# Thirteen gathered chunks are brought row by row by SyncE instead of by GpSimd

## The chip, the cores and the metric

The kernel runs on one core of one Trainium2 chip. The metric is the device time of one execution in microseconds. The engines are called PE (TensorE), DVE (VectorE), ACT (ScalarE), POOL (GpSimd) and SP (SyncE). Here SP does nothing but issue DMAs and read numbers into its registers. Each engine takes its instructions strictly in the order in which they were written.

## The reference

A graph of N = 6250 nodes and E = 100000 edges (`src`, `dst`, sorted by `dst`) passes through two layers of a graph isomorphism network, then a residual addition and a layer norm. Node features are 256 wide, hidden ones 512 wide, all in float32.

```python
def _gin_agg(h, src, dst, eps, n_nodes):
    agg = jax.ops.segment_sum(h[src], dst, num_segments=n_nodes)
    return (1.0 + eps) * h + agg

h = _gin_agg(x, src, dst, eps1, n)
h = jax.nn.relu(h @ W1a + b1a)
h = jax.nn.relu(h @ W1b + b1b)
h = _gin_agg(h, src, dst, eps2, n)
h = jax.nn.relu(h @ W2a + b2a)
out = h @ W2b + b2b
x = _layernorm(x + out, axis=-1)
```

## The kernel before

The edges are cut into chunks of 128. The destinations are skewed towards low node numbers, so the work is split in two. The seven node tiles of 128 nodes with the most edges ("heavy") are summed as matrix products: a table of counts (how many edges lead from one node to another) times the rows of all nodes. For all other chunks the 128 source rows are gathered, and a one-hot matrix on PE adds them up by destination.

**Gathers.** One chunk is one indirect DMA on POOL (`gather`, line 507): 128 rows of 1 KB from `x` in layer 1, 128 rows of 2 KB from `h1` (layer 1's result, in DRAM; `h` or `h_60` in the rows) in layer 2. They land in a ring of six pieces of up to four chunks each (`early`, in layer 2 also `late`), so that POOL can be 24 chunks ahead of the sums. PE adds a chunk up at line 1172; the merged sum of a group goes through `split` (lines 1216 to 1226) and a second product (line 1235), and DVE adds it to the tile's sum (`acc`, line 1245).

**Heavy tiles.** In layer 2 the counts come back from DRAM one table at a time (`ci<-counts`, line 1557, five buffers), ACT casts each into `cf` (line 1571, four buffers), the rows of four node tiles come as `xr<-h` (1 MB, line 1460) and are halved by ACT and DVE (lines 1532 to 1537), PE multiplies (line 1644), and DVE adds to `whole_acc` (line 1589). The heavy tiles' own rows come as `sown<-h` through one buffer (`sowing`), and DVE adds them at line 1622; each `sown` load waits until DVE is done with the one before it.

**Dense part.** Each block of node tiles is transposed (line 1289), goes through two products (lines 1342 and 1375) and is stored; in layer 2 its residual rows come as `r<-in_x` and its result goes out as `out_dram<-r`. The start value of a tile that is summed by gathers comes as `acc<-h` and is scaled by ACT (line 1002).

**Order.** A planner at build time (`Plan`) plays the engines with costs and writes the instructions of each engine in the order that comes out. It knows PE, DVE, ACT and POOL; an issue on SP costs nothing in it. SP's order is the order in which the planner came to each transfer.

**Row by row.** In layer 1 the last chunk of four groups is not gathered by POOL. SP reads 16 source numbers into registers (two `TENSOR_LOAD`s, line 2092), issues 16 DMAs of one row each into `b2b_c` (line 2098), rests in the plan for 14 us, and so on until 128 rows are there; the next chunk waits for the sum of the one before it.

```python
            def ferrying():
                yield ("rest", FERRY[0])
                n = FERRY[3]
                for g in ferries:
                    c = members[g][-1][0]
                    for o in range(0, P, n):
...
                        for j, v in enumerate(rows_in):
                            nc.sync.dma_start(b2b_c[o + j : o + j + 1, :], x[bass.ds(v, 1), :])
                        yield ("rest", FERRY[1])
```

Every DMA that SP or ACT issues takes the next of eight completion semaphores in turn, and waits until the DMA that had this one before has landed.

## Time and profile before

| what | value |
|---|---|
| time, median of 3 runs | 1304.05 us (1303.57 to 1305.85) |
| time of the profiled execution | 1301.3 us |
| its span, first to last instruction | 1299.5 us |
| busy PE / DVE / ACT / POOL | 1186.0 / 877.5 / 621.5 / 954.9 us |
| gathers on POOL | 490 in layer 1, 494 in layer 2 |
| row DMAs on SP | 512, all in layer 1 |
| mean granted PE clock | 0.962 of 2.4 GHz |

The span is what the profile shows; the device time of the same execution is 1.8 us longer. All rows and sums here are of this one execution, which is 2.75 us below the median. Busy time alone says little, because PE and POOL are both busy through most of the span; what counts is who waits for whom in which stage. SP has no busy time in the profile, as its issues are not counted, so it is read from its own timeline.

### The profile page before, as it was taken

The page shows a single profiled execution, that of the slowest core. Times are in us where ns is not written, and L with a number is a line of the kernel's source. Part 1 is how long each engine was busy: PE and PEld are TensorE (multiplying, and loading weights), DVE is VectorE, ACT ScalarE, POOL GpSimd, SP SyncE. Part 2 cuts the span into 40 slices and gives each one's busy share as a digit, 9 for nine tenths or more (in the row PEclk, how much of TensorE's full clock was granted, in tenths as well). Part 3 has the DMA queues.
Part 4 walks back from the last instruction along what each step waited for, and adds up shares of the span by engine and source line. Part 5 has one row for each costly group of instructions (what it writes and reads, how often), then busy time and mean ns, then how long its engine had stood idle before and what let it go on. Part 6 is the DMA issues. An engine that isn't in the chain of part 4 may idle for free.

```text
span 1299.5 us, 20725 instructions
## 1 busy us (share of the span) xinstructions
PE 1186.0 (91%) x6125; PEld 768.3 (59%) x6125; DVE 877.5 (68%) x2085; ACT 621.5 (48%) x1140; POOL 954.9 (73%) x997
## 2 busy tenths in 40 slices
PE   6879888889889989899788999899999999999987
PEld 4445455555455545455445677667776676766667
DVE  7997985878687979832156787678866665644334
ACT  6227766467646654674264453434343444432212
POOL 6777777777777777777777677777777777777770
PEclk9889999999999999899789899899999999999999
DMA  7446666567666665776599998898898899877771
GB/s 219 151 142 211 198 201 203 180 209 226 190 186 208 206 215 163 240 247 204 185 343 340 318 313 257 268 292 279 268 312 274 296 299 301 295 245 236 244 229 39
DMA packets 161978, 306.35 MB, mean 236 GB/s; under 512 B 26137, under 2 KB 94127, under 8 KB 161860
## 3 DMA queue, kind: packets, MB, share of 16 engines
q0 software_dynamic: 63040, 193.79, 47.9%
q1 hardware_dynamic: 77866, 86.72, 20.4%
q10 hardware_dynamic: 20954, 24.45, 5.4%
q8 instruction: 52, 0.85, 0.3%
q14 instruction: 66, 0.54, 0.1%
HBM read 274.42 MB, written 30.44 MB: 235 GB/s over the span
## 4 chain that ended last, share of the span: by engine, by line
PE 48%; DMA 17%; DVE 14%; ACT 8%; issue 6%; POOL 3%; SPq 2%; ACTq 1%; DVEq 1%; POOLq 0%
PE bank L1342 13%; PE bank L1375 10%; PE bank L1644 9%; PE bank L1172 7%; PE bank L1235 4%; DVE at L2074 3%; PE bank L1783 3%; DMA ci<-counts 3%; DMA late<-h,places 2%; DMA acc<-h 2%; DVE acc L1245 2%; DMA counts<-ci 2%; POOL early L507 2%; DVE cb L1857 2%; PE bank L1889 2%
## 5 line engine op out<-in xcount | busy, mean ns | idle before, releaser
L507 POOL DMA_INDIRECT early<-in_x_dram,srcs x490 | 481.5, 983 | 152.8 <-issue 132.0
L507 POOL DMA_INDIRECT early<-h,places x238 | 226.7, 953 | 75.4 <-issue 63.7
L507 POOL DMA_INDIRECT late<-h,places x232 | 221.9, 956 | 72.1 <-issue 57.3
L1245 DVE SCALAR_TENSOR_TENSOR acc<-bank,mask,acc 128x256 f32<-128x256 f32 (+1 forms) x360 | 205.1, 605 | 47.2 <-PE bank L1235 44.3
L1375 PE MATMUL bank<-w1b_s,ht 128*128 128x512 f32 (+1 forms) x392 | 188.8, 608 | 1.4 <-ACT ht L1352 0.8
L1342 PE MATMUL bank<-zt,w2a_s 128*128 128x256 f32 (+2 forms) x736 | 154.8, 364 | 0.2 <-ACT zt L1301 0.2
L1172 PE MATMUL bank<-early,sel 128*32 128x256 f32 (+1 forms) x1480 | 130.8, 468 | 24.1 <-DMA early<-h,places 8.5
L1644 PE MATMUL bank<-upper,cf 128*128 128x512 f32 (+1 forms) x343 | 148.8, 434 | 1.9 <-ACT upper L1532 1.1
L1342 PEld LDWEIGHTS bank<-zt,w2a_s 128*128 128x128 f32 x736 | 131.2, 193 | 24.1 <-issue 4.2
L1644 PE MATMUL bank<-xr,cf 128*128 128x512 f32 (+1 forms) x343 | 137.4, 401 | 1.1 <-DVE xr L1537 1.1
L2074 DVE TENSOR_TENSOR at<-bank,at 128x490 f32 x174 | 115.8, 666 | 28.3 <-ACT cf L1731 16.4
L1235 PE MATMUL bank<-split,to 128*128 128x256 f32 (+3 forms) x340 | 104.1, 426 | 18.8 <-DVE split L1226 6.9
L1026 DVE TENSOR_TENSOR sel<-iota,slot 128x256 f32<-128x256 f32 (+2 forms) x116 | 50.7, 437 | 98.4 <-PE bank L1172 95.0
L1375 PEld LDWEIGHTS bank<-w1b_s,ht 128*128 128x128 f32 (+1 forms) x392 | 74.2, 193 | 72.0 <-issue 60.7
L1342 PE MATMUL bank<-zt,w1a_s 128*128 128x256 f32 (+2 forms) x432 | 106.1, 397 | 9.4 <-ACT ht L1352 5.4
L1571 ACT CAST cf<-ci 128x512 fp32r<-128x512 uint16 (+1 forms) x91 | 54.1, 595 | 125.6 <-PE bank L1644 103.3
L1783 PE MATMUL bank<-xh,cf 128*128 128x512 f32 (+1 forms) x343 | 103.6, 438 | 9.3 <-DVE xh L1710 9.2
L1889 PE MATMUL bank<-cb,ca 128*128 128x490 f16 x288 | 86.0, 389 | 19.9 <-DVE at L2074 8.2
L1342 PEld LDWEIGHTS bank<-zt,w1a_s 128*128 128x128 f32 x432 | 84.2, 214 | 33.4 <-ACT ht L1352 6.3
L1172 PEld LDWEIGHTS bank<-early,sel 128*32 128x32 f32 x1480 | 40.2, 111 | 106.6 <-issue 62.5
L1710 DVE TENSOR_TENSOR xh<-bank,xh 128x512 fp32r<-128x512 f32 (+1 forms) x100 | 66.8, 672 | 43.1 <-ACT bank L1708 43.0
L1857 DVE TENSOR_SCALAR cb<-numbers,spot 128x490 f16<-128x490 f16 x288 | 90.7, 356 | 6.6 <-PE bank L1889 6.4
(193 smaller groups left out, 1764.0 us busy)
## 6 DMA issues: line engine op xcount, KB each, us to landing
raw<-in_x_dram SPq DMA_DIRECT2D x48, 512.0 KB
h<-h1r ACTq DMA_DIRECT2D x48, 256.0 KB
xr<-h SPq DMA_DIRECT2D x11, 1024.0 KB
counts<-ci ACTq DMA_DIRECT2D x84, 128.0 KB
ci<-counts SPq DMA_DIRECT2D x84, 128.0 KB
acc<-h SPq DMA_DIRECT2D x18, 512.0 KB
b2b_c<-in_x_dram SPq DMA_DIRECT2D x512, 1.0 KB
early<-in_x_dram,srcs POOLq DMA_INDIRECT x490
```

Source lines behind the costliest of these rows:

```text
L507: nc.gpsimd.indirect_dma_start(out=rows_[:, j, :], out_offset=None, in_=table, in_offset=bass.IndirectOffsetOnAxis(ap=rows_in[:, c - first ...
L1172: mm = nc.tensor.matmul(pm[b * SLOTS : (b + 1) * SLOTS], sel[:, c - groups[g][0], :], rows_[:, l, :], start=(c == part[0]), stop=(c == par ...
L1235: nc.tensor.matmul(pu[:, i * width : (i + 1) * width], to[:used], split[:used, l, :], start=(once or l == 0), stop=(once or l == 1),)
L1245: nc.vector.scalar_tensor_tensor(acc[t], pu[:, i * width : (i + 1) * width], mask[:, t - lo[g], g : g + 1], acc[t], op0=ALU.mult, op1=ALU.add,
L1342: nc.tensor.matmul(ph[:, (f - o) * TILES * P : (f - o) * TILES * P + nb], wa[:, k, f * P : (f + 1) * P], zt[:, k, :nb], start=(k == 0), st ...
L1375: nc.tensor.matmul(po[:m], ht[:, f, i * P : i * P + m], wb[:, f, :], start=(f == 0), stop=(f == KH - 1),)
L1644: nc.tensor.matmul(bank[token.number][:, :width], cf[:m, j, :], of[:m, j, :], start=(j == 0 and of is upper), stop=(j == len(ks) - 1 and o ...
L1710: begun_with["halves"] = nc.vector.tensor_tensor(xh[:m, two, 1, :], ap, xh[:m, two, 0, :], op=ALU.subtract)
L1783: nc.tensor.matmul(bank[tokens[i].number][:, : 2 * width], cf[:m, j, :], xh[:m, j, :, :].rearrange("p a d -> p (a d)"), start=(k == 0), st ...
L1857: made = nc.vector.tensor_scalar(token.tile, numbers, spot[:, c : c + 1], None, op0=ALU.is_equal)
L1889: mm = nc.tensor.matmul(bank[token.number][:, : NT * W], a.tile[:, c % BATCH, :], b.tile, start=(j == 0), stop=(j == n - 1),)
L2074: nc.vector.tensor_tensor(to, bank[token[0].number][:, : NT * W].rearrange("p (k w) -> p k w", w=W), to, op=ALU.add,)
```

## The change

- Layer 1: six chunks instead of four come row by row. 32 numbers are read at a time instead of 16, and the rest in the plan is 20 us for 32 rows instead of 14 us for 16.
- Layer 2: seven chunks, which POOL gathered before, come row by row in 28 batches of 32 rows of 2 KB from `h1`. They land by turns in the first 512 columns of `srcs` and of `dstf`, which hold the sources and destinations and are not read by layer 2. Their row numbers are first copied from `places2` to a small DRAM tile `rows2` by seven DMAs.
- So that the general path (taken when the data breaks a bound) still finds them, both tiles are stored to DRAM (`lent`) after layer 1, 256 KB each, and read back on that path alone.
- POOL issues 488 gathers in layer 1 and 487 in layer 2. PE does the same sums as before.

```diff
@@ -48,7 +48,9 @@
 PATIENT = 16.0
 SOWN2 = 25.0
 WEIGHT2 = 4.0
-FERRY = (45.0, 14.0, 5.0, 16, 610.0)
+FERRY = 32, 20.0, 5.0
+FERRY_FROM = (40.0, 5.0)
+FERRY_TO = (612.0, 596.0)
 LEAD = 1.5
 LATE = (6, 8)
 HASTE = -20.0
@@ -465,20 +467,30 @@
     FORETOLD = range(min(lo[g] for g in FORES), max(hi[g] for g in FORES) + 1)
     orders = {1: list(reversed(range(BEGIN[0], NG)))}
     orders[2] = FORES + [g for g in reversed(range(BEGIN[1], NG)) if g not in FORES]
-    ferries, t, free = [], FIRST, FERRY[0]
-    for g in orders[1]:
-        n = len(members[g])
-        t += GATHERS[0] * n
-        ready = free + FERRY[1] * P / FERRY[3] + FERRY[2]
-        if ready <= t + LANDINGS[0] and t < FERRY[4] and members[g][-1][0] < full:
-            ferries.append(g)
-            t -= GATHERS[0]
-            free = t + LANDINGS[0] + FERRY[2]
+    ferries = {}
+    for number, order in orders.items():
+        ferries[number], free = [], [FERRY_FROM[number - 1]] * number
+        t, until = (FIRST, HASTE)[number - 1], FERRY_FROM[number - 1]
+        for g in order:
+            t += GATHERS[number - 1] * len(members[g])
+            ready = max(until, free[0]) + FERRY[1] * P / FERRY[0]
+            if (
+                ready + FERRY[2] <= t + LANDINGS[number - 1] and t < FERRY_TO[number - 1]
+                and members[g][-1][0] < full and not (number == 2 and g in FORES)
+            ):
+                ferries[number].append(g)
+                t -= GATHERS[number - 1]
+                until = ready
+                free = free[1:] + [t + LANDINGS[number - 1] + FERRY[2]]
+    rows2 = dram.tile([len(ferries[2]), P], I32, name="rows2")
+    lent = [
+        (t[:, :H], dram.tile([P, H], t.dtype, name=f"lent{i}")) for i, t in enumerate((srcs, dstf))
+    ]
     pieces = {
         number: [
             (g, chunks[i : i + BURST])
             for g in order
-            for chunks in [members[g][: -1 if number == 1 and g in ferries else None]]
+            for chunks in [members[g][: -1 if g in ferries[number] else None]]
             for i in range(0, len(chunks), BURST)
         ]
         for number, order in orders.items()
@@ -1152,8 +1164,8 @@
                     for i in some:
                         yield ("until", selected[pieces[number][i][0]])
                         yield ("until", arrived[i])
-                        if once and i == last[pieces[1][i][0]] and pieces[1][i][0] in ferries:
-                            yield ("until", ferried[pieces[1][i][0]])
+                        if i == last[pieces[number][i][0]] and pieces[number][i][0] in ferried:
+                            yield ("until", ferried[pieces[number][i][0]])
                     for i in some:
                         gs = turn_of[pieces[number][i][0]]
                         if gs[0] not in shared:
@@ -1178,11 +1190,11 @@
                             if l == 0:
                                 together(mm, reads[1:])
                         last_sum[i] = mm
-                        if once and i == last[g] and g in ferries:
+                        if i == last[g] and g in ferried:
                             c, b = members[g][-1]
                             part = [c_ for c_, b_ in members[g] if b_ == b]
                             nc.tensor.matmul(
-                                pm[b * SLOTS : (b + 1) * SLOTS], sel[:, c - groups[g][0], :], b2b_c,
+                                pm[b * SLOTS : (b + 1) * SLOTS], sel[:, c - groups[g][0], :], by_row[g],
                                 start=(c == part[0]), stop=True,
                             )
                             plan.then(landed[g].set)
@@ -2083,26 +2095,43 @@
             permits = Room(plan, SIDE, False)
             if once:
                 begun = [Event(plan) for _ in STEPS]
+            ferried = {g: Event(plan) for g in ferries[number]}
+            landed = {g: Event(plan) for g in ferries[number]}
+            by_row = [b2b_c] if once else [t.bitcast(F32) for t, _ in lent]
+            by_row = {g: by_row[i % len(by_row)] for i, g in enumerate(ferries[number])}
+
             def ferrying():
-                yield ("rest", FERRY[0])
-                n = FERRY[3]
-                for g in ferries:
-                    c = members[g][-1][0]
+                n = FERRY[0]
+                if not once:
+                    for i, g in enumerate(ferries[2]):
+                        c = members[g][-1][0] - NC2
+                        nc.sync.dma_start(
+                            rows2[i : i + 1, :].rearrange("a b -> b a"), places2[:, c : c + 1]
+                        )
+                yield ("rest", FERRY_FROM[number - 1] - plan.now)
+                for i, g in enumerate(ferries[number]):
+                    if i >= number:
+                        yield ("until", landed[ferries[number][i - number]])
+                    c = members[g][-1][0] * P
+                    listed = src[c : c + P].rearrange("(a b) -> a b", a=1) if once else rows2[i : i + 1, :]
                     for o in range(0, P, n):
                         _, rows_in = nc.values_load_multi_w_load_instructions(
-                            src[c * P + o : c * P + o + n].rearrange("(a b) -> a b", a=1),
-                            engines=[mybir.EngineType.SP], min_val=0, max_val=N - 1,
+                            listed[:, o : o + n], engines=[mybir.EngineType.SP],
+                            min_val=0, max_val=N - 1 if once else N,
                             skip_runtime_bounds_check_because="an edge comes from a node",
                         )
                         for j, v in enumerate(rows_in):
-                            nc.sync.dma_start(b2b_c[o + j : o + j + 1, :], x[bass.ds(v, 1), :])
+                            nc.sync.dma_start(
+                                by_row[g][o + j : o + j + 1, :], table[bass.ds(v, 1), :]
+                            )
                         yield ("rest", FERRY[1])
                     plan.at(plan.now + FERRY[2], ferried[g].set)
-                    yield ("until", landed[g])
-                nc.sync.dma_start(b2b_c, b2b.partition_broadcast(P))
-
-            ferried = {g: Event(plan) for g in ferries}
-            landed = {g: Event(plan) for g in ferries}
+                if once:
+                    yield ("until", landed[ferries[1][-1]])
+                    nc.sync.dma_start(b2b_c, b2b.partition_broadcast(P))
+                    for t, keeps in lent:
+                        yield ("rest", 8.0)
+                        nc.sync.dma_start(keeps, t)
 
             def fetching():
                 yield ("rest", WEIGHTS if once else SOWN2 - plan.now)
@@ -2113,6 +2142,7 @@
                         yield ("rest", WEIGHT2)
 
             plan.start(fetching())
+            plan.start(ferrying())
             grouped = [b for b in range(len(blocks)) if any(uses[t] for t in blocks[b])]
             if once:
                 for i in range(PIECES):
@@ -2121,7 +2151,6 @@
                 plan.start(seeding([b for b in range(len(blocks)) if b not in grouped], wanted))
                 plan.start(selecting())
                 plan.start(counting())
-                plan.start(ferrying())
                 first_products()
             else:
                 second_products(list(reversed(range(len(ranges))))[AHEAD2:])
@@ -2184,6 +2213,8 @@
         w2a_s, w2b_s, b2b_s, fetch = second(after)
         for _ in fetch():
             pass
+        for t, keeps in lent:
+            nc.sync.dma_start(t, keeps)
         acc1 = [gdram.tile([ROWS, D], F32, name=f"acc1_{k}") for k in range(NACC)]
         acc2 = [gdram.tile([ROWS, H], F32, name=f"acc2_{k}") for k in range(NACC)]
```

The planner's cost of SP is still nothing, so the batches stand between SP's other issues where their planned times fall. SP at the second batch of layer 2, before (`w2a_s` are layer 2's first weights):

```order
L1460 DMA sown<-h_60 128x512
L756 DMA w2a_s<-in_L_gnn_W2a_dram 128x512
L1460 DMA xr<-h_60 128x4x512
L1557 DMA ci_7990<-counts 128x512
L756 DMA w2a_s<-in_L_gnn_W2a_dram 128x512
L1557 DMA ci_8031<-counts 128x512
L1460 DMA sown<-h_60 128x512
```

The same place on SP after the change (`ISA` sets an address, and 32 pairs of it and a row DMA stand there):

```order
L1472 DMA sown<-h_60 128x512
L768 DMA w2a_s<-in_L_gnn_W2a_dram 128x512
L2118 TENSOR_LOAD rows_74
L2124 ISA
L2124 DMA srcs<-h_60 1x512
...
L1472 DMA xr<-h_60 128x4x512
L1569 DMA ci_8954<-counts 128x512
L768 DMA w2a_s<-in_L_gnn_W2a_dram 128x512
L1569 DMA ci_8995<-counts 128x512
L1472 DMA sown<-h_60 128x512
```

A whole batch now stands ahead of `xr` and of the next `sown`. A little later on SP, before (`w2b_s` are the second weights):

```order
L759 DMA w2b_s<-in_L_gnn_W2b_dram 128x2x256
L1557 DMA ci_8128<-counts 128x512
L759 DMA w2b_s<-in_L_gnn_W2b_dram 128x2x256
L1557 DMA ci_8161<-counts 128x512
L1460 DMA sown<-h_60 128x2x512
```

and after the change:

```order
L771 DMA w2b_s<-in_L_gnn_W2b_dram 128x2x256
L1569 DMA ci_9092<-counts 128x512
L2118 TENSOR_LOAD rows_74
L2124 ISA
L2124 DMA srcs<-h_60 1x512
...
L771 DMA w2b_s<-in_L_gnn_W2b_dram 128x2x256
L1569 DMA ci_9222<-counts 128x512
L1472 DMA sown<-h_60 128x2x512
```

The third batch stands ahead of the following `sown`. On DVE and PE the order around these loads is the one of before. Between the first and the last batch of layer 2 SP has 161 other DMAs to issue.

## Rows read from the trace of the kernel before

**Rows 1.** Groups by line, POOL: busy, mean ns, idle before, releasers.

```profile
L507 POOL DMA_INDIRECT early<-in_x_dram,srcs x490 | 481.5, 983 | 152.8 <-issue 132.0 <-DMA early<-in_x_dram,srcs 4.6 <-DVE srcs L645 3.7
L507 POOL DMA_INDIRECT early<-h,places x238 | 226.7, 953 | 75.4 <-issue 63.7 <-DMA early<-h,places 4.9 <-PE bank L1172 3.2
```

**Rows 2.** Windows: length, PE, PEld, DVE, ACT, POOL busy (count), clock, DMA share, GB/s.

```profile
625.00:650.00 25.00, 18.74 (x95) 12.27 (x92) 1.56 (x3) 6.29 (x18) 18.20 (x20) 0.73 0.59 195
700.00:725.00 25.00, 18.41 (x79) 12.35 (x78) 16.25 (x28) 9.27 (x17) 19.05 (x20) 0.86 1.04 380
950.00:975.00 25.00, 25.00 (x130) 19.42 (x129) 15.31 (x30) 10.58 (x21) 18.91 (x21) 1.00 0.92 310
1250.00:1275.00 25.00, 21.45 (x146) 16.70 (x147) 5.94 (x15) 5.47 (x15) 11.00 (x12) 0.93 0.54 173
```

**Rows 3.** Waits of PE in layer 2, 640 to 1300: total, times, longest.

```profile
PE bank L1172 <- DMA early<-h,places: 8.5, 5, 4.4
PE bank L1172 <- DMA late<-h,places: 1.3, 1, 1.3
```

**Rows 4.** SP's number reads, line 2092: duration ns min/median/max, first and last start.

```profile
L2092 SPq TENSOR_LOAD <-in_src_dram x32: 1724/1972/3207, 17.2 to 523.7; - x32
```

**Rows 5.** Timeline of SP in layer 1, two batches of 16 rows: start, duration.

```profile
294.88 6.45 SPq L2098 DMA_DIRECT2D b2b_c<-in_x_dram  x16
...
468.57 8.59 SPq L2098 DMA_DIRECT2D b2b_c<-in_x_dram  x16
```

**Rows 6.** Timeline of SP at the layers' border.

```profile
595.72 3.69 SPq L1557 DMA_DIRECT2D ci<-counts  x2
640.25 0.93 SPq L1460 DMA_DIRECT2D xr<-h  x2
...
664.49 0.79 SPq L1460 DMA_DIRECT2D apart<-h  x2
667.93 15.52 SPq L1557 DMA_DIRECT2D ci<-counts  x6
685.87 0.32 SPq L1460 DMA_DIRECT2D sown<-h  x1
686.24 0.42 SPq L756 DMA_DIRECT2D w2a_s<-in_L_gnn_W2a_dram  x1
...
692.65 0.32 SPq L1460 DMA_DIRECT2D sown<-h  x1
...
707.85 0.43 SPq L759 DMA_DIRECT2D w2b_s<-in_L_gnn_W2b_dram  x1
...
713.74 0.37 SPq L1460 DMA_DIRECT2D sown<-h  x1
```

**Rows 7.** Chain that ended last: start, duration, what.

```profile
692.65 11.62 DMA sown<-h
705.07 6.54 DMA sown<-h
```

**Rows 8.** Timeline of DVE at the `sown` additions: start, duration, idle before.

```profile
704.29 0.75 DVE L1622 SCALAR_TENSOR_TENSOR whole_acc<-sown,e,whole_acc 128x512 f32<-128x512 f32 x1 [6.19 <-DMA sown<-h]
...
724.06 0.74 DVE L1622 SCALAR_TENSOR_TENSOR whole_acc<-sown,e,whole_acc 128x512 f32<-128x512 f32 x1
```

**Rows 9.** Timeline of PE just behind those additions.

```profile
705.76 1.92 PE L1172 MATMUL bank<-late,sel 128*32 128x512 f32 x16 [0.58 <-DVE acc L1245]
...
716.24 0.79 PE L1235 MATMUL bank<-split,to 128*128 128x512 f32 x1 [6.00 <-DVE split L1226]
```

**Rows 10.** Timeline of POOL behind that.

```profile
729.28 0.94 POOL L507 DMA_INDIRECT early<-h,places  x1 [3.19 <-PE bank L1172]
```

**Rows 11.** Waits of ACT in layer 1, 50 to 560.

```profile
ACT xh L1701 <- DMA raw<-in_x_dram: 19.3, 6, 5.4
...
ACT acc L1002 <- DMA acc<-in_x_dram: 16.4, 5, 7.1
```

**Rows 12.** Waits of ACT in layer 2, 700 to 1250.

```profile
ACT acc L1002 <- DMA acc<-h: 17.2, 6, 5.9
```

## The prediction

> **What bounds the kernel now.** I read the groups by line first, then windows of 25 us, then the waits of PE and the timeline of SP. POOL's gathers cost 481.5 + 132.0 us of busy time and issue for 490 in layer 1, 1.25 us each, and 226.7 + 63.7 us for 238 in layer 2, 1.22 us each [rows 1]. So the 13 gathers that the change takes from POOL are 2 x 1.25 = 2.5 us in layer 1 and 7 x 1.22 = 8.5 us in layer 2. The windows say whether POOL sets the pace. At the end of layer 1 it does: from 625 to 650 PE is busy for 18.74 us of 25 and POOL goes on with 20 instructions. In layer 2 it does not: from 950 to 975 PE is busy for 25.00 us of 25 [rows 2]. All that PE waits for gathers in layer 2 is 8.5 + 1.3 = 9.8 us in six waits [rows 3]. That is the most that layer 2 can gain from fewer gathers, as PE's sums stay the same.
>
> One stretch of layer 2 has PE idle for another reason: 700 to 725, 18.41 us busy at a granted clock of 0.86 and with the DMA engines at a share of 1.04, full [rows 2]. The chain of waits names it: a `sown` load is issued at 692.65 and lands after 11.62 us [rows 7]. DVE has waited 6.19 us for it when it adds it at 704.29 [rows 8], PE waits 0.58 us for DVE's `acc` at 705.76 and 6.00 us for DVE's `split` at 716.24 [rows 9], and POOL then waits 3.19 us for PE's sum, its ring being full [rows 10]. What delays this `sown` delays DVE, then PE, then POOL, with no slack between.
>
> **The change part by part.**
>
> *What a batch costs SP.* A read of numbers takes 1.97 us in the middle of 32, 1.72 at least [rows 4]. Sixteen row DMAs took 6.45 us in one batch and 8.59 in another [rows 5], so 32 take 12.9 to 17.2 us. The old batch has two reads in a row. The new one in layer 2 has one (its order shows a single `TENSOR_LOAD` ahead of the rows), so a batch is 14.9 to 19.2 us of SP; I take 16.4, nearer to the lower end, since a row waits only when SP's eight completion semaphores are all under way. A row of 2 KB, twice those of layer 1, is not in the trace; below, the price is that of 1 KB, above, that of the slower batch.
>
> *Layer 1.* Minus 2.5 us, as POOL sets its end. Against it, other loads on SP stand behind 32 rows instead of 16, up to 8.59 us more. ACT already waits 19.3 us for `raw` and 16.4 us for `acc` loads there [rows 11], 35.7 us over 32 batches, 1.1 us a batch. This is hidden by POOL's lead of 24 chunks, 24 x 1.25 = 30 us; without it ACT would be late by up to 8.59 us at a time. I cost it at nothing, with 0 to 8 us as bounds.
>
> *The border.* The seven copies into `rows2` and the two stores of 256 KB are nine DMAs at 0.3 to 0.5 us each by SP's rows, some 4 us. SP issues nothing from 599.4 (595.72 + 3.69) to 640.25 [rows 6], which covers the stores and, since `places2` is there early, the copies too; without that cover 4 us would be on `xr`. Nothing.
>
> *First batch of layer 2.* It stands behind the two `apart` loads at 664.49, ahead of the six `ci` that SP now issues over 15.52 us from 667.93 [rows 6]: one at a time, as buffers come free, so five tables are ahead of ACT. A batch until about 682 leaves SP the time to issue them before 685.87. Nothing; if those tables are wanted sooner than I think, up to 682 - 667.93 = 14 us on ACT's casts, which I count among the upper bounds of the forecast.
>
> *Second batch of layer 2.* In the order it stands behind the first `w2a_s` and ahead of `xr`, two `ci`, a `w2a_s` and the critical `sown`. That `w2a_s` is issued at 686.24 and done at 686.66 [rows 6], so the batch occupies SP until 686.7 + 16.4 = 703.1, and the five issues behind it (0.3 to 0.5 us each, 1.8 together) put the `sown` at 704.9 instead of 692.65, 12.2 us later. It may land in less than 11.62 us, because the transfers ahead have drained: the next one took 6.54 us [rows 7], which takes 5.1 us off, so 7.1 is the lower bound. If the issues behind the batch again take the 6 us that they take now (686.66 to 692.65), it is 12.2 + 4.2 = 16.4. I take 12.2. DVE has no slack there [rows 8], so PE gets all of it: plus 12.2 us.
>
> *Third batch.* It stands behind the `w2b_s` ahead of the one issued at 707.85 and ahead of the `sown` issued at 713.74 [rows 6]. Without a batch this `sown` waits until DVE has freed the buffer. With one, SP reaches it at about 707.3 + 16.4 + 0.9 = 724.6, counted on the present times, 10.9 us later. Landing after 6.54 us it would now be there at 720.3, and DVE uses it at 724.06 [rows 8], a slack of 3.8 us. DVE loses 7.1 us. PE shows no wait of its own behind this addition, so between 0 and 7.1 reach it; I take 4.
>
> *The later 25 batches.* In layer 2 ACT waits 17.2 us for `acc` loads, in six waits up to 5.9 us [rows 12]: these loads come just in time, and each that now falls behind a batch is up to 16.4 us late. The ring covers it as long as POOL's lead holds. Layer 1 has carried such batches with ACT's waits of 1.1 us each; 25 x 1.1 = 27 us of ACT is the upper bound, 0 the lower. As ACT is not what PE waits for in most stretches (10.58 us busy of 25 in 950 to 975 [rows 2]), I take 4 us on PE.
>
> *Gathers of layer 2.* PE's waits for gathers, 9.8 us, vanish, since 8.5 us of POOL and the later PE give POOL the lead: minus 9.8.
>
> *Sum.* -2.5 + 12.2 + 4 + 4 - 9.8 = +7.9 us on the profiled execution's 1301.3 us, 1309.2. It lies 2.75 us under the median of 1304.05, so against the median it is 1312.
>
> *A price on the DMA engines.* A row lies in one partition and is 2 KB; a batch is 64 KB, and in 582 us of 28 batches it is one each 20.8 us. No view here shows which of the 16 engines carries it. If all rows go through one, then in 25 us at 310 GB/s [rows 2] each engine moves 7.75 MB / 16 = 484 KB, and that one 77 KB more, 16%: at a share of 0.92 it would be asked for 1.07. The Trainium skill ("DMA: Bandwidth & Descriptors", section "Why a DMA increments its semaphore by 16 and not by 1") says just this: a transfer issued by SP is spread over as many engines as divide its outer dimension, and one of a single row uses one, the lowest-numbered. By that rule rival D holds; by the mean share alone the rows are 1% of the bytes and cost nothing. The same page, section "Issuing engines are not separate DMA queues", speaks against the change as well: the engine that starts a transfer saves only its own issue time, so moving gathers from POOL to SP frees POOL alone and no bandwidth. The shares of 0.92 to 1.04 agree that bandwidth is scarce.
>
> **The rivals.**
>
> A. *The loads are absorbed, faster.* The `sown` behind the drained queue is issued at 704.9 but lands in 6.5 us or less, the third batch and the `acc` loads fall into slack, and PE's 9.8 us of waits go. Sum -2.5 + 7.1 - 9.8 = -5.2, and with no lateness at all -12.3: 1292 to 1299, say 1297. It decides as soon as the lateness that reaches PE is under 12.3 us in all. For it speaks that PE's order has 24 chunks of lead; against it, DVE's idle 6.19 us ahead of just that load.
>
> B. *A wash*, lateness of 10 to 15 us in all: 1301.5 to 1306.5.
>
> C. *SP runs out of time.* From 667.93 [rows 6] to about 1250, when POOL has 12 instructions left [rows 2], SP has 582 us. It needs 161 x 0.45 = 72 us for the other issues (0.32 to 0.49 us each [rows 6]) and 28 x 16.4 = 459 for batches, 531 in all. Above 510 / 28 = 18.2 us a batch it is late, and PE waits at the sum of the row-wise chunk while `ci`, `xr` and `acc` queue behind the rows. At 19.2 us this is 28 us by the end: 1304.05 + 28 = 1332. The slow batch of 8.59 us for 16 rows [rows 5] speaks for it, the fast one against it.
>
> D. *One DMA engine becomes the bound*: 0.07 x 582 = 39 us of lateness in every wide load at most. Half of it inside slack leaves 20 on 1304.05, 1324.
>
> E. *The change doesn't take the gathers off POOL*: excluded, 488 and 487 are issued.
>
> **How the numbers follow.** The forecast (plus 2.6 to plus 16 us, 1306.7 to 1320) has 0.36, A 0.28, B 0.14, C 0.13, D 0.09. About 0.2%, 2.6 us, is what a measurement of this kernel can tell from no change. So faster 0.28, same 0.14, slower 0.58. The predicted time is that of the likeliest case, 1312. The range leaves out the better part of A with all of the lateness gone and the far part of C: 1293 to 1334. The forecast's own range is 1306.7 to 1320.
>
> **What would show it.** In the changed profile: on SP's timeline, a batch of 32 rows in layer 2 in 13 to 17 us, none issued over 18.2 us in the mean (else C). At the second batch, `sown` issued near 705 and DVE's idle time ahead of its addition near 18 us instead of 6.19, PE's busy time from 700 to 730 well under 18.41 in 25 (else A). PE's waits for gathers in layer 2 near nothing instead of 9.8 us. Layer 1's end 2.5 us earlier. ACT's waits for `acc` in layer 2 above 17.2 us. Wide loads that take longer to land all through layer 2, beside a DMA share that is no higher, would speak for D; PE's waits at the row-wise sums for C. The prediction is wrong if the order around the first `sown` loads does not stretch (another wait on SP already covered the batch), or if a row costs SP far from 0.4 to 0.54 us.

## The result, and the profile after

The changed kernel takes 1639.02 us (median of 4 runs, 1629.92 to 1647.84), the kernel before 1304.05 us in the same set: a ratio of 1.2565, 95% interval 1.249 to 1.264. The forecast was 1312, its range ended at 1334.

In three of the five sets of runs further down the kernel before itself took 1656 to 1689 us, so each run is given against the kernel before of its own set, and sizes of a loss in microseconds are taken from the other two sets, where that took 1304 and 1301 us.

Groups by line of the changed kernel, POOL, which answers to [rows 1] (columns as there):

```profile
L519 POOL DMA_INDIRECT early<-in_x_dram,srcs x488 | 476.6, 977 | 314.9 <-PE bank L1184 164.4 <-issue 129.2 <-PE bank L1196 4.2
L519 POOL DMA_INDIRECT early<-h,places x235 | 225.2, 958 | 168.4 <-PE bank L1184 100.7 <-issue 61.3 <-DMA early<-h,places 2.7
```

POOL has its gathers off, as the change says, but now stands 164.4 us in layer 1 and 100.7 us in one half of layer 2 behind PE's sums: its ring is full. Not POOL is late, PE is. Windows of the changed kernel, one in layer 1 and three in layer 2 (columns as in [rows 2]):

```profile
500.00:600.00 100.00, 68.48 (x331) 38.61 (x323) 59.67 (x151) 42.74 (x73) 54.70 (x55) 0.85 0.48 147
875.00:900.00 25.00, 13.47 (x56) 8.37 (x57) 15.23 (x26) 8.84 (x16) 13.19 (x14) 0.69 0.88 300
1100.00:1125.00 25.00, 18.14 (x82) 13.45 (x83) 7.17 (x14) 7.31 (x13) 7.52 (x8) 0.76 0.50 144
1300.00:1325.00 25.00, 23.39 (x131) 15.89 (x131) 12.29 (x25) 9.05 (x18) 15.09 (x16) 1.00 0.66 225
```

PE, which was busy for 25.00 us of 25 in the middle of layer 2 before [rows 2], is now busy for 54% to 94% of these windows. Three of the four have DMA shares of 0.48 to 0.66, and only the one behind the first `sown` loads still has 0.88. Over the layers the DMA share fell too, from 0.65 to 0.52 in layer 1 (15 to 600 before, 20 to 740 after) and from 0.88 to 0.70 in layer 2 (640 to 1260, 820 to 1600). So for most of the time nothing that moves data or computes is the bound.

PE's stalls come with a lower clock. The granted clock is 1.00 where PE is busy for 23.39 us of 25 and 0.69 where it is busy for 13.47; in the mean it fell from 0.962 to 0.875 of 2.4 GHz, and the same 6125 matmuls keep PE busy for 1241.7 us instead of 1186.0. Up to 56 us of the loss may lie there; no run separates them.

The waits of ACT in layer 1 (20 to 740) and in layer 2 (820 to 1600) of the changed kernel say for what (total, times, longest):

```profile
ACT xh L1713 <- DMA raw<-in_x_dram: 87.1, 10, 12.5
ACT acc L1014 <- DMA acc<-in_x_dram: 72.1, 7, 12.4
...
ACT acc L1014 <- DMA acc<-h: 147.5, 14, 24.0
```

In layer 1 159.2 us where the kernel before had 35.7 [rows 11], in layer 2 147.5 where it had 17.2 [rows 12], all of it for loads that SP issues. PE's longest waits in layer 2 (820 to 1600) are in turn for ACT, 109.8 us in all, where they were 1.8 us in the kernel before (640 to 1260); the two largest:

```profile
PE bank L1247 <- ACT split L1236: 62.1, 7, 12.5
PE bank L1387 <- ACT ht L1364: 33.9, 3, 19.5
```

The chain that ended last agrees. Its shares of the span, first before, then after the change (14% of the 23% on SP are row DMAs, 7% are reads):

```profile
PE 48%; DMA 17%; DVE 14%; ACT 8%; issue 6%; POOL 3%; SPq 2%; ACTq 1%; DVEq 1%; POOLq 0%
PE 34%; SPq 23%; DMA 17%; issue 10%; DVE 7%; ACT 6%; POOL 2%; ACTq 1%; DVEq 0%; POOLq 0%
```

What SP does in it, by its rows (line L2118 reads, duration in ns min/median/max; then its timeline at the second batch of layer 2):

```profile
L2118 SPq TENSOR_LOAD <-rows x28: 3838/6484/10763, 818.9 to 1540.8; - x28
L2118 SPq TENSOR_LOAD <-in_src_dram_ptr x24: 1195/2050/3500, 15.6 to 716.3; - x24
...
L2118 SPq TENSOR_LOAD <-in_src_dram x24: 3316/3626/5447, 17.0 to 718.3; - x24
```

```profile
849.92 0.42 SPq L768 DMA_DIRECT2D w2a_s<-in_L_gnn_W2a_dram  x1
856.92 13.38 SPq L2124 DMA_DIRECT2D srcs<-h  x32
870.42 0.41 SPq L1472 DMA_DIRECT2D xr<-h  x1
...
872.52 0.79 SPq L1472 DMA_DIRECT2D sown<-h  x1
```

and DVE at that `sown`, which answers to [rows 8]:

```profile
883.66 0.75 DVE L1634 SCALAR_TENSOR_TENSOR whole_acc<-sown,e,whole_acc 128x512 f32<-128x512 f32 x1 [21.90 <-DMA sown<-h]
...
911.91 0.75 DVE L1634 SCALAR_TENSOR_TENSOR whole_acc<-sown,e,whole_acc 128x512 f32<-128x512 f32 x1 [12.45 <-DMA sown<-h]
```

A batch holds SP from 850.4 to 870.30 (856.92 + 13.38), 20 us: the read took 6.3 us here, the rows 13.38. DVE waits 21.90 us instead of 6.19.

SP's time by kind, from its trace: each instruction with the gap ahead of it is put to its line; what remains are gaps ahead of other DMAs, mostly SP's waits for buffers. A gap that reaches over the edge of a stretch counts with the instruction behind it, so in layer 2 a line of the table misses the length of its stretch by up to 22 us.

| stretch | rows | reads | other issues | waits ahead of them |
|---|---|---|---|---|
| before, layer 1 (15 to 600) | 257 | 139 | 50 | 138 |
| after, layer 1 (15 to 738) | 383 | 149 | 57 | 134 |
| before, layer 2 (640 to 1260) | 0 | 0 | 90 | 552 |
| after, layer 2 (818 to 1600) | 387 | 185 | 92 | 97 |

Layer 1 is 138 us longer (738 - 15 less 600 - 15), which is what rows and reads gained (126 + 10). That reads as if SP's time were simply used up, though a fifth of the stretch is still waits. The experiments were made to see whether that is so.

### The profile page after: what moved, and what is told of

The parts are those of the page before. It is cut to its first block, busy times and chain, and to the rows that moved or that the text cites. A ratio compares the mean times of both kernels' runs of the same rounds, so it can differ in the third digit from the quotient of the medians.

```text
span 1640.8 us, 24224 instructions
## 1 busy us (share of the span) xinstructions
PE 1241.7 (76%) x6125; PEld 800.1 (49%) x6125; DVE 876.1 (53%) x2085; ACT 619.2 (38%) x1140; POOL 943.7 (58%) x988
## 4 chain that ended last, share of the span: by engine, by line
PE 34%; SPq 23%; DMA 17%; issue 10%; DVE 7%; ACT 6%; POOL 2%; ACTq 1%; DVEq 0%; POOLq 0%
SPq L2124 14%; PE bank L1387 9%; PE bank L1354 8%; SPq L2118 7%; PE bank L1184 5%; PE bank L1656 4%; DMA acc<-h 4%; DMA raw<-in_x_dram 3%; PE bank L1795 3%; PE bank L1247 3%; PE bank L1901 2%; DVE acc L1257 2%; POOL early L519 2%; DMA out_dram<-r 1%; DMA acc<-in_x_dram 1%
## 5 line engine op out<-in xcount | busy, mean ns | idle before, releaser
L519 POOL DMA_INDIRECT early<-in_x_dram,srcs x488 | 476.6, 977 | 314.9 <-PE bank L1184 164.4
L519 POOL DMA_INDIRECT early<-h,places x235 | 225.2, 958 | 168.4 <-PE bank L1184 100.7
L519 POOL DMA_INDIRECT late<-h,places x228 | 217.2, 952 | 141.6 <-PE bank L1184 75.8
L1387 PE MATMUL bank<-w1b_s,ht 128*128 128x512 f32 (+1 forms) x392 | 194.4, 626 | 25.1 <-ACT zt L1313 24.3
L1247 PE MATMUL bank<-split,to 128*128 128x256 f32 (+3 forms) x340 | 116.7, 466 | 108.5 <-ACT split L1236 62.1
L1184 PE MATMUL bank<-early,sel 128*32 128x256 f32 (+1 forms) x1470 | 135.7, 485 | 51.5 <-DVE at L2086 22.9
L1656 PE MATMUL bank<-upper,cf 128*128 128x512 f32 (+1 forms) x343 | 155.5, 453 | 8.2 <-DVE whole_acc L1601 8.0
L1795 PE MATMUL bank<-xh,cf 128*128 128x512 f32 (+1 forms) x343 | 111.8, 465 | 47.4 <-DVE xh L1722 47.4
L1247 PEld LDWEIGHTS bank<-split,to 128*128 128x128 f32 (+1 forms) x340 | 71.8, 220 | 145.0 <-ACT split L1236 65.2
L1387 PE MATMUL bank<-w2b_s,ht 128*128 128x256 f32 (+1 forms) x336 | 97.5, 419 | 57.7 <-ACT ht L1364 33.9
L1014 ACT ACTIVATE acc<-acc,e 128x512 f32<-128x512 f32 (+2 forms) x44 | 36.3, 842 | 220.0 <-DMA acc<-h 147.5
```

The source lines that it names most:

```text
L519: nc.gpsimd.indirect_dma_start(out=rows_[:, j, :], out_offset=None, in_=table, in_offset=bass.IndirectOffsetOnAxis(ap=rows_in[:, c - first ...
L1184: mm = nc.tensor.matmul(pm[b * SLOTS : (b + 1) * SLOTS], sel[:, c - groups[g][0], :], rows_[:, l, :], start=(c == part[0]), stop=(c == par ...
L1247: nc.tensor.matmul(pu[:, i * width : (i + 1) * width], to[:used], split[:used, l, :], start=(once or l == 0), stop=(once or l == 1),)
L1387: nc.tensor.matmul(po[:m], ht[:, f, i * P : i * P + m], wb[:, f, :], start=(f == 0), stop=(f == KH - 1),)
L1656: nc.tensor.matmul(bank[token.number][:, :width], cf[:m, j, :], of[:m, j, :], start=(j == 0 and of is upper), stop=(j == len(ks) - 1 and o ...
L1795: nc.tensor.matmul(bank[tokens[i].number][:, : 2 * width], cf[:m, j, :], xh[:m, j, :, :].rearrange("p a d -> p (a d)"), start=(k == 0), st ...
```

## Experiments

Theory SP: SP's time is used up, and what is added to it is added to the kernel. Rival block: it is each load's standing behind one block of rows that counts, even where SP has time left. Further rivals: the order of instructions, the row transfers, the border.

**Each layer alone.** `FERRY_TO` shuts one layer off; `e_l2` has layer 1 as before. The edit of `e_l1`:

```diff
-FERRY_TO = (612.0, 596.0)
+FERRY_TO = (612.0, -1000000.0)
```

> Only layer 1 is changed (six chunks, 32 rows a batch); layer 2 gathers as before. Theory SP (SP has no time left: in the changed profile layer 1 holds 383 us of rows, 149 us of number reads, 57 us of other issues and 134 us of waits, in the kernel before 257, 139, 50 and 138, so what is added to rows and reads is added to the time): layer 1 ends about 135 us later and the kernel takes 1430 to 1450 us. Rival block (a batch of 32 only makes single loads up to 9 us late): at most 24 x 4 us of that reaches the end, under 1400. Rival gate (layer 1 as forecast, no loss): 1302, and the whole loss is layer 2's.

> Only layer 2 is changed; layer 1 brings four chunks in batches of 16 rows as before. Theory SP: 28 batches cost SP 6.5 us for the read and 13.8 us for 32 rows, 570 us in all, beside 92 us of other issues and some 100 us of waits that do not vanish: layer 2 takes about 160 us longer, 1460 to 1500 us. Rival carried over (layer 2 only suffers because layer 1 ended late and disturbed it): under 1350.

`e_l1` took 1464.4 us (160 over the 1303.92 of the kernel before), `e_l2` 1487.04 (183 over), one execution each. `e_l1` is above theory SP's 1450 and far above the rival's 1400; `e_l2` is where theory SP put it. Together 343, the whole change 335: two losses that add up, and neither is carried from one layer to the other.

**Without the reads, and without the rows.** `e_l2_oneread` reads 32 numbers once and uses them for every batch of layer 2; `e_l2_whole` brings 32 neighbouring rows by one DMA. Neither brings the rows that the sums need. The edit of `e_l2_whole`, cut to its heart (`once` is layer 1):

```diff
-                        for j, v in enumerate(rows_in):
...
+                        if not once:
+                            nc.sync.dma_start(by_row[g][o : o + n, :], table[o : o + n, :])
+                        for j, v in enumerate(rows_in if once else []):
```

> As the run with only layer 2 changed, but the 32 numbers are read once and used for all 28 batches, so the sums use wrong rows. Theory SP: 28 x 13.8 + 92 + 100 = 578 us of SP, which fits into the 620 us that the layer took before: 1300 to 1330 us. Rival one DMA engine (the rows of one partition overload one DMA engine): the rows are as many and as large, so nothing changes against the run with the reads, 1460 to 1500. Rival reads only (the rows cost nothing, only the reads do): 1295.

> As the run with only layer 2 changed, but each batch is one DMA of 32 rows that stand together in h, without a read, so the sums use wrong rows. SP is nearly free then, POOL has seven gathers fewer as in the change. Theory SP: what is left is the gain of POOL's relief, up to 9.8 us of PE's waits for gathers: 1294 to 1304. Rival order (the changed order of the instructions costs by itself): above 1310.

`e_l2_oneread` took 1414.06 us (1.0873, interval 1.0816 to 1.0929), `e_l2_whole` 1312.04 (1.0089, 1.0055 to 1.0123). So of the 183 us about 73 go with the reads and 102 more with the rows; the bytes, POOL's relief and the new order cost 8. Theory SP missed twice. For `e_l2_oneread` it had 578 us of need fit into 620 and so 1300 to 1330. SP's table there (640 to 1380): rows 485, read 8, other issues 90, and 172 us of waits that did not go away. The rows alone are dearer than the 381 us that they took in `e_l2`, so all in all SP is held for 73 us less. For `e_l2_whole` theory SP had a gain, 1294 to 1304, and the rival of the written order, above 1310, fits. `e_l2_whole` also shows what POOL's relief is worth. PE's waits for gathers in its layer 2 (640 to 1310):

```profile
PE bank L1184 <- DMA early<-h,places: 6.1, 4, 3.0
...
PE bank L1184 <- DMA late<-h,places: 1.2, 2, 1.0
```

7.3 us with seven gathers fewer, against 9.8 [rows 3]: they are waits for landings, hardly for POOL's pace.

**Reads as filler, small blocks, block size in layer 1, and the border.** `e_l2_readonly` reads twice per batch and brings 30 rows by one DMA, two singly; `e_l2_blocks8` has `FERRY` of 8 rows and 5 us with one read in all; `e_l1_blocks` has layer 1's four chunks at 32 rows and 28 us; `e_l2_whole_bare` drops the stores to `lent` and the copies to `rows2`. In `FERRY` the first three numbers are layer 1's, the next three layer 2's. The edit of `e_l1_blocks`, without what it shares with `e_l2`:

```diff
-FERRY = 32, 20.0, 5.0
...
-FERRY_TO = (612.0, 596.0)
+FERRY = ((32, 28.0, 5.0), (32, 20.0, 5.0))
...
+FERRY_TO = (610.0, -1000000.0)
```

> Only layer 2 changed; per batch two reads of 32 numbers, two row DMAs and one DMA of 30 rows that stand together, so the sums use wrong rows. SP is held for 2 x 6.5 + 1.2 = 14 us a batch, about as long as by the 32 rows of the run with one read (16 us, 1414 us), but with hardly any DMAs. Theory SP (SP's own time is what is short, whatever fills it): 1370 to 1420. Rival traffic (it is the row DMAs, on one DMA engine or in the way of wide loads): near the run with whole batches, 1312, up to 1325.

> Only layer 2 changed, the 32 numbers read once (the sums use wrong rows), but eight rows every 5 us in the plan instead of 32 every 20 us. Theory SP time: as many rows cost SP as much, 1400 to 1425 as with blocks of 32. Rival block (what hurts is that a load falls behind 14 us of rows at a time, so that it comes late): a block is 3.5 to 4 us, and it takes under 1350.

> Layer 1 alone, four chunks as before, but in batches of 32 rows every 28 us instead of 16 rows every 14 us; layer 2 gathers as before. 16 x 5.6 = 90 us of reads instead of 32 x 4.3 = 139, the same 257 us of rows. Theory SP time: SP has 49 us more, nothing is lost, 1295 to 1306. Rival block: loads come up to 8 us later and it takes over 1312.

> As the run with whole batches in layer 2 (1312 us; wrong rows), but without the two stores to lent and the seven copies to rows2. In that run the first gather of layer 2 started 9 us later than before, and the last one at the same time. Theory border (those nine DMAs delay the step from layer 1 to layer 2): 1300 to 1305. Rival order (the written order of layer 2 is worse): 1310 to 1314.

In this set the kernel before took 1656.44 us. Against it: `e_l2_blocks8` 1.086 (1.0768 to 1.0951), `e_l1_blocks` 1.0506 (1.0427 to 1.0585), `e_l2_whole_bare` 0.9911 (0.9874 to 0.9947). `e_l2_readonly` ran twice, 1693.9 and, in the profiled execution, 1665.4 us. There it holds SP for 11.8 us a batch (reads 280, all three DMAs of a batch together 52, by 28), nearly without row DMAs, and takes 1.4% more than `e_l2_whole_bare` (1642.18 us), 0.8 us a batch. Neither theory's number can be read off in this set, and two executions so far apart are thin ground: a hold of 12 us seems to cost little, whatever fills it. The last two were measured again, `e_l1_blocks` twice:

> The run with four chunks in batches of 32 rows every 28 us in layer 1 again; on the chip where it ran first the kernel before itself took 1656 us, and this one 5% more. Theory SP time: 49 us less of reads than before, nothing lost, 1295 to 1306 where the kernel before takes 1304. Rival block: loads come later behind the longer blocks, over 1312.

> Four chunks in layer 1 in 16 batches of 32 rows every 28 us, with the 512 rows of the kernel before and 49 us less of reads; layer 2 without rows. Theory block: a block of 22 us instead of 12 costs 5.6 to 6.5 us of the end each, 16 times, 90 to 104 us: 1390 to 1410. Rival SP time: nothing lost, 1295 to 1306.

> Whole batches without the stores to lent and the copies to rows2, again (on the chip where it ran first it was 0.9% faster than the kernel before). Theory border (those nine DMAs cost the 8 us that whole batches lost): 1294 to 1304. Rival order (layer 2's written order costs them): 1310 to 1314.

1.0477 (1.0402 to 1.0551), 1.0492 (1.0423 to 1.056), and 0.9989 (0.9942 to 1.0036), in sets where the kernel before took 1685.72 and 1688.65. `e_l1_blocks` is the clearest sign for the rival: the 512 rows of the kernel before, fewer reads, nothing changed in layer 1 but 32 instead of 16 rows at a time and the two stores to `lent` at its end, and 5% lost three times. The traces of one set show it directly. In `e_l2_rest40` (further down), which has layer 1 as before, SP is held for 32 x 18.1 = 579 us there and the last gather of layer 1 starts at 836 us; in `e_l1_blocks_b` it is held for 16 x 33.2 = 531 us, 48 us less, and that gather starts at 916, 80 us later. The size of the loss where the kernel before takes 1304 us was not measured. The border's part stays open: `e_l2_whole` was 0.9% slower than the kernel before, and without the nine DMAs it is 0.1% to 0.9% faster, but no set has both.

**No rows at all, and rows with time to spare.** `e_none` lets POOL gather everything; `e_l2_rest40` brings three chunks in layer 2, in batches 40 us apart in the plan. First in a set where the kernel before took 1685.72:

> No chunk comes row by row in either layer; POOL gathers all, four more in layer 1 than before. Theory POOL (before, POOL sets layer 1's end: it idles 8 us only beside its issue): 4 x 1.25 = 5 us slower, 1307 to 1311. Rival SP (SP is already what sets layer 1's pace before: 396 of its 585 us are rows and reads): it gets faster, under 1299.

> Layer 1 as before; in layer 2 three chunks instead of seven, 12 batches of 32 rows, 40 us apart in the plan. SP has 12 x 20 = 240 us of rows and reads in layer 2. Theory SP time: whole batches cost 8 us more than before at 11 us of SP, one read 110 at 493, all reads 183 at 566, so the last 73 us of SP cost 73 us of time, and with that slope the loss begins at about 390 us of SP. At 240 nothing of it is left but the border's 8 us: 1300 to 1315. Rival block (each batch makes the loads behind it late, however much time SP has): 12 x 5 us and more, over 1350.

0.9593 (0.9516 to 0.967) and 1.0587 (1.0511 to 1.0662). Then, with two neighbours, in a set where it took 1301.28 (the edit of `rest40_b`):

```diff
-FERRY = 32, 20.0, 5.0
...
+FERRY = ((16, 14.0, 5.0), (32, 40.0, 5.0))
```

> The run with one read for all batches of layer 2 again (110 us over the kernel before where that took 1304 us), as the neighbour of the next one on the same chip. Both theories: 100 to 120 us over the kernel before, if that takes 1304 us here; 145 to 200 where it takes 1650 and more.

> The same rows and the same one read, but eight rows every 5 us of the plan instead of 32 every 20 us. Theory SP time: as slow as its neighbour with blocks of 32, within 15 us. Rival block: a load waits behind 4 us of rows instead of 16, and at least half of the neighbour's loss is gone.

> Three chunks in layer 2, 12 batches of 32 rows, 40 us apart in the plan; layer 1 as before. Where the kernel before takes 1304 us, SP has 12 x 20 = 240 us of rows and reads among some 550 us of waits. Theory SP time: nothing lost beyond the border's 8 us, 1300 to 1318. Rival block: each batch costs what it cost in the run with seven chunks, 183 / 28 = 6.5 us, 12 x 6.5 = 78 us, 1370 to 1390; half of it, 1340, would say that both are at work.

> No row by row at all, again (4% faster than the kernel before on the chip where it ran first and rows cost SP twice as much). Where the kernel before takes 1304 us: theory POOL 1307 to 1311, as POOL sets layer 1's end and gets four gathers more; rival SP (rows hold back layer 1 in the kernel before too) under 1300.

`oneread_b` 1424.39 (1.093, 1.0854 to 1.1005), `blocks8_b` 1379.72 (1.0587, 1.0512 to 1.0662), `rest40_b` 1368.81 (1.0503, 1.0409 to 1.0597), `none_b` 1304.65 (1.0021, 0.9996 to 1.0046). `none_b` lies between its two forecasts (1307 to 1311, and under 1300): where the kernel before takes 1301 us, its own rows in layer 1 cost nothing and win nothing that is clear of the noise.

`rest40_b` decides against theory SP as I had it. SP's table in its layer 2 (640 to 1330) has rows 164, reads 69, other issues 106 and 369 us of waits, time enough, and the loss is 67.5 us. It is a miss for the rival's price too, 78, but a near one. How one batch costs is seen there. SP's timeline:

```profile
772.89 0.43 SPq L1281 DMA_DIRECT2D r<-in_x_dram  x1
783.24 13.32 SPq L2124 DMA_DIRECT2D srcs<-h  x32
796.66 0.36 SPq L1569 DMA_DIRECT2D ci<-counts  x1
797.12 0.41 SPq L1472 DMA_DIRECT2D acc<-h  x1
```

ACT's, DVE's and PE's behind it (start, duration, in brackets the idle time before and what ended it):

```profile
803.44 1.15 ACT L1014 ACTIVATE acc<-acc,e 128x1024 f32<-128x1024 f32 x1 [13.82 <-DMA acc<-h]
804.50 0.60 ACT L1544 CAST upper<-xr 128x512 fp32r<-128x512 f32 x1
805.00 0.58 ACT L1545 COPY bank<-xr 128x512 f32<-128x512 f32 x1
...
805.62 0.69 DVE L1549 TENSOR_TENSOR xr<-bank,upper 128x512 fp32r<-128x512 f32 x1 [12.85 <-ACT bank L1545]
...
806.51 1.94 PE L1184 MATMUL bank<-late,sel 128*32 128x512 f32 x8 [10.83 <-ACT zt L1313]
```

The `acc` load stands behind the batch and is issued at 797.12. ACT's next instruction scales it and waits 13.82 us. Behind it in ACT's order stand casts and copies that have nothing to do with `acc` (`upper`, `bank`, `zt`), and DVE (12.85 us) and PE (10.83 us) wait for those. One late load stops ACT, and ACT stops the rest. In `rest40_b` ACT waits so seven times in layer 2:

```profile
ACT acc L1014 <- DMA acc<-h: 58.6, 7, 14.3
```

The load is issued late; it does not travel longer. From issue to the last update of its semaphore, by the traces, an `acc<-h` load takes 6.84 us in the middle in layer 2 of `rest40_b`, 6.93 in the changed kernel and 8.03 in the kernel before; for `ci<-counts` it is 5.91, 5.07 and 5.75, for the 13 `xr<-h` 9.45, 9.58 and 8.63. Only `xr` lands later, by 1 us, so a slowing of the wide transfers by the rows does not carry the loss.

Loss for one block against the time that a block holds SP, less the 8.1 us of `e_l2_whole` in layer 2 (hold: rows and reads of SP's table by the number of blocks). A block is what stands on SP without another instruction between: of the 112 batches of `blocks8_b` some stand right behind one another, which leaves 76 blocks, and of the 28 of `oneread_b` two do:

| run | blocks | hold, us | loss for one, us |
|---|---|---|---|
| `blocks8_b` | 76 | 6.9 | (78.4 - 8.1) / 76 = 0.9 |
| `oneread_b` | 27 | 18.2 | (123.1 - 8.1) / 27 = 4.3 |
| `rest40_b` | 12 | 19.4 | (67.5 - 8.1) / 12 = 5.0 |
| `e_l2` | 28 | 20.2 | (183.1 - 8.1) / 28 = 6.3 |
| `e_l1` | 24 | 22.1 | 160.5 / 24 = 6.7 |

Twelve blocks with SP half idle cost 5.0 us each (3.8 to 5.8 by the interval of `rest40_b`), 28 with far less of SP's time left 6.3: the loss goes with the number and the hold of the blocks, and hardly with what is left of SP's time. It grows faster than the hold: for one microsecond of hold 0.13 us in `blocks8_b`, 0.23 to 0.31 in blocks of 32. The kernel before, with 32 blocks of 396 / 32 = 12.4 us in layer 1, loses nothing that is clear of `none_b`. Small blocks do not make it free: `blocks8_b` keeps 78 of its neighbour's 123 us, so theory SP (as slow as the neighbour) and the rival (at least half gone) both missed there. SP is held for 522 us in it, no less than in `oneread_b` (492). What keeps those 78 us was not tested.

**Past the batches.** `rest40_act` is `rest40_b` with the `acc` and `sown` loads of layer 2 issued by ACT (17 of 23 `acc` and 5 of 6 `sown` loads moved).

```diff
-                    in_rows(ts, a, table, where)
+                    in_rows(ts, a, table, where, nc.sync if once else nc.scalar)
...
-                            in_rows(ts, s, h1, place)
+                            in_rows(ts, s, h1, place, nc.scalar)
```

> The run with three chunks in layer 2 (67 us over the kernel before, of which ACT waits 58.6 us for acc loads and DVE 27.8 us for sown), but the acc and sown loads of layer 2 are issued by ACT instead of SP, so that none of them stands behind a batch; the batches on SP are the same 12. Theory block, by its late acc and sown loads: ACT's waits for acc fall under 20 us, and at least half of the loss goes, 1304 to 1335. Rival contention (the row DMAs slow the transfers themselves, wherever they are issued): no change, 1360 to 1375. Rival other loads (ci, xr and the stores behind a batch carry it): 1340 to 1365.

1796.13 us in a set where the kernel before took 1688.65: 1.0652 (1.0571 to 1.0733), not better than `e_l2_rest40`'s 1.0587. The theory of blocks expected at least half of the loss to go, and missed. Its sign came: compared with `e_l2_rest40` ACT's waits for `acc<-h` loads fell from 43.4 us to none that is listed and DVE's for `sown` from 31.2 to none. But the loss stayed, and ACT now waits for another load that still stands behind the batches, which is not listed in `e_l2_rest40`:

```profile
ACT upper L1544 <- DMA xr<-h: 44.5, 4, 20.5
```

So the waits for `acc` and `sown` are one way of the loss and not the only one; that `xr` took their place fits the rival of the other loads, but no run moved all loads past the batches, so this last step is argued and not shown. No version here is faster than the kernel before beyond the interval.

## Why the prediction was wrong

- **A batch, 16.4 us (14.9 to 19.2).** Measured 20.4 in layer 2 (387 + 185 us by 28): rows 13.8, inside 12.9 to 17.2, and 2 KB is not dearer than 1 KB; the read 6.48 us in the middle where I took 1.97. The term was mis-sized because [rows 4] is a read of 16 numbers and the new one is of 32. In layer 1 a batch is 22.1, as two reads stand there, one of them of a pointer, also not in those rows.
- **Second and third batch, 12.2 + 4 us.** Right in kind. DVE's wait at the first `sown` is 21.90 us (18 forecast), and the load lands after 11.12 us, near the 11.62 that was taken; behind the third batch it is 12.45 us (7.1 forecast). This stretch was seen because the trace of before had an idle time there.
- **The later 25 batches, 4 us on PE, 0 to 27.** The step that failed. I argued that ACT "is not what PE waits for in most stretches", from its 10.58 us of busy time in 25. ACT takes its instructions in order, so a late `acc` holds everything behind it. ACT waited 147.5 us for `acc` loads in layer 2, and PE 109.8 us for ACT, 62.1 + 33.9 of it for `split` and `ht`, against 1.8 us before. Layer 2's loss is 183 us, where this term had 4 and its upper bound 27.
- **Layer 1, minus 2.5 us and loads late by 0 to 8.59.** Failed in the same way. The 24 chunks of POOL's lead were named as cover; they cover a late POOL, not a late `raw` on the way through ACT and DVE to PE: POOL's ring was full, and it waited 164.4 us for PE's sums. Loss 160 us, where this term had 0 to 8. That 32 batches of 16 rows cost ACT 1.1 us each did not carry over to blocks nearly twice as long (159.2 / 24 = 6.6 us).
- **The border, nothing.** `e_l2_whole` loses 8 us with SP free, and its first gather of layer 2 starts at 647.8 instead of 638.4, but its last one at 1262.7 instead of 1263.4, so POOL has made up the late start by then. What the 8 us are was not settled.
- **Gathers, minus 9.8 us.** In the changed kernel PE's waits for `places` gathers are gone from the list, as forecast, but only because PE is late itself. With SP free (`e_l2_whole`) 7.3 of the 9.8 us stay when POOL has seven gathers fewer: there was next to nothing to win.
- **Rival C** had the right engine, and its sign came, batches of over 18.2 us in the mean, but at the wrong price: 28 us at 19.2 us a batch. At the measured 20.4 its sum gives 28 x 2.2 = 62 us, not 183. That SP's waits are in part waits for engines that wait for SP, and so are not free time, is the likely reason; it is argued and not shown.
- **Rival D** was right that a row goes over one DMA engine: by the traces the kernel before moves 512 packets of 1 KB more than `none_b`, one for each of its 512 rows. Its price did not come. Wide loads land no later but for 1 us of `xr` (the figures at `rest40_b`), and with one read the same rows go over the same engines and 73 us are gone.

The chance of slower, 0.58, was right in sign. The range was by far too narrow, since no case let a late load stop an engine and all that stands behind it in that engine's order: they priced single loads, SP's time as a budget, or the transfers.

## What to carry to other kernels

An in-order queue that issues loads just in time has no room that its idle time shows: price a block put into it by the loads right behind it, by the engine that waits for each, and by everything that this engine has queued behind that wait. Blocks cost more than in proportion to their length, so what was free at 12 us says little about 20. And an operation that is made larger, as a read of 32 numbers instead of 16, needs its own row or a bound from two sizes.

## What the hardware showed that was not expected

A read of 32 numbers into SP's registers takes 3.63 us in the middle from the kernel's input and 6.48 us (3.84 to 10.76) from a DRAM tile in the busier layer 2, against 1.97 for 16. A row DMA costs SP 0.50 us at 1 KB (383 us for 768) and 0.43 at 2 KB (387 for 896) in the changed kernel, but 0.54 and 0.57 at 2 KB in `e_l2_oneread` and `blocks8_b` (485 and 514 us for 896), where no reads stand between the rows. Of the 0.43 us the DMA instruction itself is 0.228.
